# A two-phase recurrent recommender: the length mask moves to gathered rows, one exponential and one transpose move ahead, and some index columns are fetched earlier

## The chip, the cores and the metric

The kernel runs on one core of a Trainium2 chip. A core has five engines with instruction queues of their own, each of which works strictly in the order of its queue: TensorE (PE; PEld is its weight loads), VectorE (DVE), ScalarE (ACT), GpSimd (POOL) and SyncE (SP), which here issues most of the transfers. Engines wait for one another through semaphores. The metric is the device time of one execution in microseconds, the median of several runs.

## The reference

1024 users each have a history of 100 item vectors of 128 numbers, a 0/1 mask of 100 entries, and a length from 1 to 100. In float32:

1. A GRU runs over the 100 items; its states are the `keys` (1024 x 100 x 128).
2. Each key gets a score by a small network of the key, the item and their product. A softmax over the masked scores gives `attn`, and `pooled = sum over t of attn * keys` (1024 x 128).
3. `att_seq = pooled.T[:100]`: an entry of a *user's* pooled vector at feature t serves as the attention weight of another user at step t, through the transposition that the reference makes.
4. A second recurrence (AUGRU) runs over the keys: `u = a_t * sigmoid(..)`, `h = (1 - u) * h + u * tanh(..)`. Of its 100 states, the one at position length - 1 is used.
5. That state, the user, the item, a masked history mean and their product go through a three-layer network with sigmoids to one number per user.

```python
att_seq = pooled.T[:T]
u = a_t[:, None] * u
h_new = (1.0 - u) * h + u * h_hat
attention_feature = jnp.take_along_axis(aug_out, idx, axis=1)[:, 0, :]
```

Since only the state at length - 1 counts, a weight of zero from there on freezes the state. So the kernel sets the weights of steps at or past a user's length to zero (the mask of lengths, `used`), sorts the users by length, longest first, and lets the second recurrence become narrower as users drop out.

## The kernel before

**Phase 1** (`gru_phase`). 1024 users are two halves of 512 columns; features lie on the 128 partitions. A loop over t = 0..99 runs the GRU step of each half (24 matmuls with 128 x 32 weights each, `gru`), scores the keys of the step before (`attend`, `take`), runs the softmax in blocks of steps as *stages* (`softmax`: scores, tops, then `exponents`, then sums), and lets POOL add up the masked history and the pooled keys. Keys are transposed on DVE in 32 x 32 blocks and stored to DRAM in `keys_d`, whose rows hold 8 steps each (4 in the first). The order of every queue is written out by hand: there is no planner.

Work for later is a generator, `load_later`: at each step of the loop that has no softmax stage, it advances to its next `yield`. It loads lengths and masks, ranks the users (each step one comparison of 1024 elements, `above`), scatters identity and place by rank into a DRAM table `inv_d`, reads it back sorted into `idx` and `idx_k` (the row numbers for later gathers), and makes the masks `used` and `used_first`, and `quad` and `low`, small columns that pick a partition's own quarter.

**The hand-over.** After the loop (from about 1372 us of the profile) the last scores, the last softmax blocks and the features of the final network are worked off. `features(g)` alternates matmuls and an ACT copy to `part` (L720); `some(6, 7)` advances features 6 and 7. `key(n, half)` transposes the keys of steps 0 and 1. Then the pooled values of the first four features (`soon`) are finished, multiplied with `used_first` into `first_w` (L1089), and sorted by two matmuls, `by_row` (L1099) and `first` (L1105), which give the state after step 0 (L1114). After that the pooled values of the other features (`rest`) are finished on DVE, multiplied with `used` (L1122) and stored by SP to `pooled_d` (L1125). At the end every engine loads the word `over_d` and branches (L1587, L1588) to one of three versions of phase 2 that differ in their widths.

**Phase 2** (`augru_phase`) runs steps 1 to 99. Up to a narrow width, each step is two `half_step(t, i)`, i = 0, 1. In such a half step PE closes `ph` of the half step before, closes `pr` and `pu` of this one, and opens three gates of the next one (`open_gates`, L1239), which needs that one's keys `k`; DVE makes `r` (L1275), the new `h` (L1277), `pu * at` (L1281) and `rest` (L1284). `load_key(t, i)` puts the keys of a step on the features' side: for t < 4 by PE, later by a DVE transpose (L1228) of rows that POOL gathers from `keys_d` by an indirect DMA (`load_row`, L189). Before such a gather, POOL copies one column of a DVE result into the row's buffer (`later["pace"]`, L188), so that gathers keep pace with the steps. The weights are gathered by POOL from `pooled_d` (`gather_weights`, L154); `store_weights` transposes them on PE (L1188, at the end of half steps (2, 1) and (3, 0)), DVE copies them out (L1190), and SP stores them to `att_d`, from where each step's row is loaded (`load_att`, L1203). `predict` is the final network, for groups of users as they drop out.

What sets the order around the change: in half step (4, 0) the keys of (4, 1) are transposed, after `rest` and right before the gates of (4, 1) are opened:

```python
if (t, i) == (FIRST[1], 0):   # FIRST[1] is 4
    load_key(t, 1)
```

Of the kernel before, what the change touches and what calls it, by code (L numbers as in the profile page):

```python
# [9 lines left out]
F32 = mybir.dt.float32  # L10
# [9 lines left out]
P = 128  # L20
B = 1024
# [63 lines left out]
def kernel(ctx: ExitStack, tc: tile.TileContext, a: dict, out: bass.AP):  # L85
# [34 lines left out]
    mask_d = dram.tile([T, B], BF16, name="mask_d")  # L120
    inv_d = dram.tile([B, 2], I32, name="inv_d")
    perm_d = dram.tile([NH, 2, HB], F32, name="perm_d")
# [16 lines left out]
    pooled = const.tile([P, NK, R], F32, name="pooled")  # L139
    idx = const.tile([P, GH, NH * 2], I32, name="idx")  # L140
    idx_k = const.tile([P, KH, NH], I32, name="idx_k")
    quad = const.tile([P, SOON], F32, name="quad")
    idx_p = const.tile([P, HB // PR], I32, name="idx_p")
    h_all = const.tile([P, NH, HB], F32, name="h_all")
# [7 lines left out]
    def gather(dst, src, g, i):  # L152

        nc.gpsimd.indirect_dma_start(  # L154
            out=dst,
            out_offset=None,
            in_=src,
            in_offset=bass.IndirectOffsetOnAxis(ap=idx[:, g, 2 * i : 2 * i + 1], axis=0),
        )
# [40 lines left out]
    def gru_phase(pools):  # L200
# [72 lines left out]
        def load_later():  # L273
# [30 lines left out]
            nc.gpsimd.iota(step_i, pattern=[[1, T]], base=0, channel_multiplier=0)  # L304
            ids = pre.tile([P, NG, 2], I32, name="ids")
            nc.gpsimd.iota(ids[:, :, 0], pattern=[[P, NG]], base=0, channel_multiplier=1)
# [16 lines left out]
            own = pre.tile([P, NG], F32, name="own")  # L323
            nc.scalar.copy(own, ids[:, :, 0])
            room = []
            for j, room_i in enumerate(rooms):
# [69 lines left out]
            nc.vector.tensor_scalar_mul(low[:, 0:1], r3, -3.0)  # L396
            nc.vector.tensor_scalar_mul(low[:, 1:2], r3, -3.0 * R)
            nc.vector.tensor_scalar_mul(r3, r3, -3.0)
            yield
            for c in range(SOON):  # L400
                nc.vector.tensor_scalar(
                    quad[:, c : c + 1], quarter, float(c * R), None, ALU.is_equal
                )
            yield
# [7 lines left out]
                out=own, in0=length, scalar=float(B), in1=own, op0=ALU.mult, op1=ALU.subtract  # L412
            )
            yield
            rank = pre.tile([P, NG], F32, name="rank")
            rank_i = pre.tile([P, NG], I32, name="rank_i")
            for g in range(NG):
# [10 lines left out]
                yield  # L428
            nc.vector.tensor_copy(rank_i, rank)
            for g in range(NG):  # L430
                nc.gpsimd.indirect_dma_start(
                    out=inv_d,
                    out_offset=bass.IndirectOffsetOnAxis(ap=rank_i[:, g : g + 1], axis=0),
                    in_=ids[:, g, :],
                    in_offset=None,
                )
                yield
# [5 lines left out]
            for i in range(NH):  # L443
# [3 lines left out]
                )  # L447
            place_i = pre.tile([P, KH, NH, 2], I32, name="place_i")
            len_k = pre.tile([P, NK], I32, name="len_k")
# [11 lines left out]

            own_place = pre.tile([P, GH, NH * 2], F32, name="own_place")
            nc.scalar.copy(own_place, idx)
            yield
            parts = pre.tile([P, 2, NH, GH], F32, name="parts")
            for i in range(NH):
                at_id, at_place = (own_place[:, :, 2 * i + j] for j in range(2))
                nc.vector.scalar_tensor_tensor(
                    out=parts[:, 0, i],
                    in0=at_id,  # L470
                    scalar=float(P // R),
                    in1=at_place,
                    op0=ALU.mult,
                    op1=ALU.subtract,
                )
                nc.vector.tensor_sub(parts[:, 1, i], at_place, at_id)
            yield
            for i in range(NH):
# [603 lines left out]
        for half in halves:  # L1082
# [6 lines left out]
        nc.vector.tensor_mul(  # L1089
            w.rearrange("p (c k) -> p k c", c=SOON),  # L1090
            pooled[:, :, soon],
            later["used_first"].rearrange("p c k -> p k c"),
        )
# [25 lines left out]
        for half in reversed(halves):  # L1119
            half.pool(T, nc.vector, rest)  # L1120
            acc = pooled[:, half.ks, :]
            nc.vector.tensor_mul(acc, acc, later["used"][:, half.ks, :])  # L1122
            to = pooled_d[half.cols, :].rearrange("(k r) f -> r k f", r=R)
# [8 lines left out]
    def augru_phase(pools, widths, alive):  # L1132
# [50 lines left out]
        def store_weights(i):  # L1183

            n = T - SOON
            p = pa.tile([P, HB], F32, tag="a", name="pw")
            for g in range(GH):
                nc.tensor.transpose(p[:n, ts(g, P)], sorted_rows[i][:, g, SOON:T], ident)  # L1188
# [65 lines left out]
        def half_step(t, i):  # L1254
# [54 lines left out]

            if (t, i) == (FIRST[1] - 1, 0):  # L1310
                load_key(t + 1, i)
# [77 lines left out]
        def predict(g, last=False):  # L1389
# [80 lines left out]
            for q in range(P // R):  # L1470
# [6 lines left out]
                )  # L1477
            all_y = later["all_y"]
            nc.vector.tensor_add(all_y, p, all_y)
            nc.sync.dma_start(  # L1480
                out=out.rearrange("(q c) -> q c", c=BQ),
                in_=all_y.rearrange("(q r) c -> q r c", r=R)[:, 0, :],
            )

# [16 lines left out]
        def earlier_results():  # L1501
            later["all_y"] = wp.tile([P, BQ], F32, tag="att_t", name="all_y", bufs=2)
            nc.sync.dma_start(
                out=later["all_y"],
                in_=early_d.rearrange("(q c) o -> q (o c)", c=BQ)
                .unsqueeze(1)
                .to_broadcast([P // R, R, BQ]),
            )
# [152 lines left out]
```

## Time and profile before

| | |
|---|---|
| median of 3 runs | 2004.55 us (2002.19 to 2005.18) |
| the profiled execution | 2006.11 us |
| its span, first to last instruction | 2004.3 us |
| mean granted clock of PE | 0.997 of full |
| busy PE / DVE / POOL / ACT | 1983.5 / 1679.0 / 1263.7 / 942.9 us |

The span is shorter than the time of its own execution by 1.8 us, which lies before the first and after the last instruction. All times below that are written like 1422.72 are microseconds from the start of the span. Busy time counts work only: waits, branches and the issuing of transfers are not in it. In the order of instructions, neighbours of one kind are joined (x4); float32 matmuls come as two passes. What stands in brackets is the engine's idle time before an instruction and what, by the semaphores, ended it; where several semaphores are waited for, it is the one that came last by the profile, which need not be the cause.

### The profile page before, as it was taken

To read this page: it belongs to the slowest core of one execution; us is meant where nothing else is said; L and a number is where in the kernel's file an instruction comes from. 1 tells how busy PE (TensorE), PEld (TensorE's weight loads), DVE (VectorE), ACT (ScalarE), POOL (GpSimd) and SP (SyncE) were. 2 spreads that over 40 slices of the span, in tenths; PEclk is the share of its full clock that TensorE was granted. 3 is DMA by queue.
4 is the path that set the end of the run, shared out by engine and by line. 5 is a ranking of instruction groups with operands and counts; after the bars stand their busy time and mean duration, and the time that the engine had idled before them with its cause. 6 is when DMAs were issued, how large, how long until landed. Compare 5 with 4: busy or idle time off the path is not lost.

```text
span 2004.3 us, 40958 instructions
## 1 busy us (share of the span) xinstructions
PE 1983.5 (99%) x15324; PEld 954.9 (48%) x15324; DVE 1679.0 (84%) x3038; ACT 942.9 (47%) x1690; POOL 1263.7 (63%) x1307
## 2 busy tenths in 40 slices
PE   9999999999999999999999999999899999999998
PEld 2345555555333333333333333345344556678997
DVE  7888989897978888888878798998677778888995
ACT  4444454454544444544444444546333444445563
POOL 0333939568796959596896868898753454445331
PEclk9999999999999999999999999999999999999999
DMA  4443333323333533333333333332542333333331
GB/s 125 98 118 92 107 106 101 93 86 102 115 106 109 117 100 117 118 114 100 104 111 107 107 92 107 103 96 77 157 130 90 101 107 98 93 103 99 84 82 33
DMA packets 244300, 205.59 MB, mean 103 GB/s; under 512 B 61538, under 2 KB 206794, under 8 KB 244090
## 3 DMA queue, kind: packets, MB, share of 16 engines
q1 hardware_dynamic: 231578, 170.29, 29.6%
q0 software_dynamic: 12224, 32.04, 5.7%
q8 instruction: 123, 2.02, 0.4%
q14 instruction: 87, 0.71, 0.1%
q10 hardware_dynamic: 288, 0.52, 0.1%
HBM read 146.73 MB, written 54.42 MB: 100 GB/s over the span
## 4 chain that ended last, share of the span: by engine, by line
PE 95%; DVE 1%; POOL 1%; DMA 1%; ACT 1%; issue 1%; SPq 0%; POOLq 0%; DVEq 0%; ACTq 0%
PE ps L569 50%; PE pm L745 17%; PE ph L1243 4%; PE pr L1239 4%; PE ph L1239 4%; PE pu L1239 4%; PE pu L1243 4%; PE pr L1243 4%; DMA rows<-keys_d,idx_k 1%; POOL rows L189 1%; PE last L712 1%; PE pr L1334 0%; PE ph L1334 0%; POOL att_r L154 0%; PE p L1454 0%
## 5 line engine op out<-in xcount | busy, mean ns | idle before, releaser
L569 PE MATMUL ps<-x,wih 128*32 128x512 f32 x4800 | 653.1, 593 | 0.0
L569 PE MATMUL ps<-hn,whh 128*32 128x512 f32 x4752 | 646.3, 592 | 1.6 <-ACT hn L617 1.6
L569 PEld LDWEIGHTS ps<-x,wih 128*32 128x32 f32 x4800 | 212.1, 110 | 315.1 <-issue 285.8
L569 PEld LDWEIGHTS ps<-hn,whh 128*32 128x32 f32 x4752 | 209.7, 110 | 311.9 <-issue 302.8
L554 POOL TENSOR_TENSOR xm<-x,m 128x512 f32<-128x512 f32 x200 | 235.8, 1179 | 143.0 <-DMA m<-mask_d 142.7
L581 ACT ACTIVATE r<-ps,brz 128x512 f32<-128x512 f32 x200 | 137.7, 689 | 387.6 <-PE ps L569 387.1
L555 POOL TENSOR_TENSOR hist<-hist,xm 128x512 f32<-128x512 f32 x200 | 257.7, 1289 | 15.7
L189 POOL DMA_INDIRECT rows<-keys_d,idx_k x218 | 211.9, 972 | 84.5 <-POOL rows L188 73.6
L675 POOL TENSOR_TENSOR pooled<-pooled,kw 128x512 f32<-128x512 f32 (+1 forms) x191 | 244.0, 1278 | 15.0
L674 POOL TENSOR_TENSOR kw<-kt,e 128x512 f32<-128x512 f32 (+1 forms) x191 | 205.1, 1074 | 67.1 <-DVE e L863 67.0
L600 ACT ACTIVATE ps<-ps,bih 128x512 f32<-128x512 f32 x200 | 132.4, 662 | 226.8 <-DVE ps L599 226.8
L745 PE MATMUL pm<-hn,wk 128*32 128x512 f32 x1200 | 228.8, 592 | 0.0
L745 PE MATMUL pm<-kq,wkq 128*32 128x512 f32 x1200 | 228.7, 592 | 0.0
L1251 ACT ACTIVATE c<-ph,bh 128x510 f32<-128x510 f32 (+57 forms) x174 | 88.3, 507 | 258.4 <-PE ph L1243 258.3
L745 PE MATMUL pm<-mv,w 128*32 128x512 f32 (+1 forms) x808 | 207.8, 592 | 0.0
L589 DVE SCALAR_TENSOR_TENSOR u<-ps,bhh,r 128x512 f32<-128x512 f32 x198 | 147.6, 745 | 69.4 <-PE ps L569 65.4
L604 DVE TENSOR_TENSOR d<-hn,ps 128x512 f32<-128x512 f32 x198 | 136.2, 688 | 35.5 <-ACT ps L600 35.3
L188 POOL COPY rows<-rest 128x1 f32<-128x1 f32 x198 | 37.5, 189 | 197.9 <-DVE rest L1284 196.5
L617 ACT COPY hn<-ps 128x512 f32<-128x512 f32 x200 | 116.5, 583 | 93.2 <-DVE kq L611 91.4
L605 DVE TENSOR_TENSOR d<-ps,d 128x512 f32<-128x512 f32 x200 | 138.4, 692 | 25.6 <-ACT ps L601 11.6
L599 DVE TENSOR_TENSOR ps<-ps,u 128x512 f32<-128x512 f32 x200 | 140.0, 700 | 22.7 <-PE ps L569 2.0
L1273 DVE TENSOR_TENSOR pu<-pu,c 128x510 f32<-128x510 f32 (+57 forms) x173 | 82.0, 474 | 80.7 <-ACT c L1251 78.5
(263 smaller groups left out, 3164.2 us busy)
## 6 DMA issues: line engine op xcount, KB each, us to landing
x<-in_hist_x SPq DMA_DIRECT2D x210, 256.0 KB
keys_d<-kt SPq DMA_DIRECT2D x48, 1024.0 KB
m<-mask_d SPq DMA_DIRECT2D x200, 128.0 KB
rows<-keys_d,idx_k POOLq DMA_INDIRECT x218, 3.0
s_b<-mv SPq DMA_DIRECT2D x200, 8.0 KB
keys_d<-kt SPq DMA_DIRECT2D x32, 64.0 KB
mask_i<-in_mask SPq DMA_DIRECT2D x8, 200.0 KB
part_d<-part SPq DMA_DIRECT2D x2, 400.0 KB
```

The source lines that it names most:

```text
L189: nc.gpsimd.indirect_dma_start(out=r[:, at, :], out_offset=None, in_=keys_d[q], in_offset=bass.IndirectOffsetOnAxis(ap=idx_k[:, k, i : i + ...
L554: nc.gpsimd.tensor_mul(d, x, m)
L555: nc.gpsimd.tensor_add(acc, acc, d)
L569: nc.tensor.matmul(p[ts(q, R), :], lhsT=w[:, g, ts(q, R)], rhs=v, start=(j == 0), stop=(j == len(parts) - 1),)
L589: nc.vector.scalar_tensor_tensor(out=u, in0=ph, scalar=bhh[:, 2:3], in1=r, op0=ALU.add, op1=ALU.mult,)
L599: nc.vector.tensor_add(pi, pi, u)
L605: nc.vector.tensor_mul(d, pz, d)
L674: eng.tensor_mul(d, k, w)
L675: eng.tensor_add(acc, acc, d)
L745: nc.tensor.matmul(p[i][s, :], lhsT=w[:, s], rhs=v, start=start, stop=stop)
L1239: nc.tensor.matmul(p, lhsT=m[:, 1, :], rhs=k, start=True, stop=False)
L1243: nc.tensor.matmul(p, lhsT=m[:, 0, :], rhs=v, start=False, stop=True)
```

## The change

- The exponential of the last softmax block (`stage(2); exponents()`) is issued ahead of the second `some(6, 7)`, whose part on ACT is two copies.
- `used` shrinks to the first four steps and a quarter of the partitions each, and replaces `used_first`; `first_w` is laid out as (k c) instead of (c k). The two multiplies of `pooled` with `used` (L1122) are gone.
- In their place `used_s`, a mask in the sorted order, is made in phase 1 from a third column of `inv_d` (the length), and `store_weights` multiplies the gathered rows with it on DVE before PE transposes them.
- `quad` and a column of `low` now come from two small index columns, made by POOL, stored to DRAM (`kc_d`) and loaded back across the partitions one stage of `load_later` later (`kc_p`), well before they are used.
- Keys of step 4: in step 3, each half step transposes its own half's; before, the second half's were transposed in (4, 0).
- In steps 1 and 2 gathers have no pacing copy.
- The results' buffer `all_y` lies in `pooled`, and the last store is issued after the generator of the last prediction instead of at its end.
- `load_later` has three `yield`s fewer.

```diff
+    kc_d = dram.tile([2, P], I32, name="kc_d")
-    idx = const.tile([P, GH, NH * 2], I32, name="idx")
+    idx = const.tile([P, GH, NH * 3], I32, name="idx")
+    used_s = const.tile([P, NH, GH, T - SOON], U8, name="used_s")
+    all_y = pooled.rearrange("p k r -> p (k r)")[:, :BQ]
...
+            nc.gpsimd.tensor_copy(ids[:, :, 2], len_i)
...
-            nc.vector.tensor_scalar_mul(low[:, 1:2], r3, -3.0 * R)
             nc.vector.tensor_scalar_mul(r3, r3, -3.0)
-            yield
-            for c in range(SOON):
-                nc.vector.tensor_scalar(
-                    quad[:, c : c + 1], quarter, float(c * R), None, ALU.is_equal
-                )
+            kc = mid.tile([1, 2, NK, SOON], I32, name="kc", **once)
+            nc.gpsimd.iota(
+                kc[:, 0], pattern=[[1, NK], [0, SOON]], base=0, channel_multiplier=0
+            )
+            nc.gpsimd.iota(
+                kc[:, 1], pattern=[[0, NK], [1, SOON]], base=0, channel_multiplier=0
+            )
+            nc.sync.dma_start(
+                out=kc_d.rearrange("j p -> (j p)").unsqueeze(0),
+                in_=kc.rearrange("o j k c -> o (j k c)"),
+            )
             yield
...
+            kc_p = pre.tile([P, 2], I32, name="kc_p")
+            nc.sync.dma_start(out=kc_p, in_=kc_d.rearrange("j p -> p j"))
             yield
...
+            kc_f = pre.tile([P, 2], F32, name="kc_f")
+            nc.scalar.copy(kc_f, kc_p)
+            nc.vector.tensor_scalar_mul(low[:, 1:2], kc_f[:, 0:1], -3.0 * R)
+            for c in range(SOON):
+                nc.vector.tensor_scalar(
+                    quad[:, c : c + 1], kc_f[:, 1:2], float(c), None, ALU.is_equal
+                )
...
+                nc.vector.tensor_tensor(
+                    out=used_s[:, i],
+                    in0=own_place[:, :, 3 * i + 2].unsqueeze(2).to_broadcast([P, GH, T - SOON]),
+                    in1=step[:, SOON:].unsqueeze(1).to_broadcast([P, GH, T - SOON]),
+                    op=ALU.is_gt,
+                )
...
-            column = pre.tile([P, R], F32, name="column")
-            nc.vector.tensor_scalar(column, step[:, :R], quarter, None, ALU.add)
-            yield
-            used_first = later["used_first"] = pre.tile([P, SOON, NK], U8, name="used_first")
-            used = later["used"] = pre.tile([P, NK, R], U8, name="used")
+            used = later["used"] = pre.tile([P, NK, SOON], U8, name="used")
             nc.vector.tensor_tensor(
                 out=used,
-                in0=last.unsqueeze(2).to_broadcast([P, NK, R]),
-                in1=column.unsqueeze(1).to_broadcast([P, NK, R]),
+                in0=last.unsqueeze(2).to_broadcast([P, NK, SOON]),
+                in1=step[:, :SOON].unsqueeze(1).to_broadcast([P, NK, SOON]),
                 op=ALU.is_gt,
             )
-            yield
-            nc.vector.tensor_scalar(
-                used_first.rearrange("p c k -> p k c"), used[:, :, :SOON], quad[:, 0:1], None, ALU.mult
-            )
+            nc.vector.tensor_scalar(quarter, quarter, 0.0, None, ALU.is_equal)
+            nc.vector.tensor_scalar(used, used, quarter, None, ALU.mult)
             yield
...
-        some(6, 7)
         stage(2)
         exponents()
+        some(6, 7)
...
         nc.vector.tensor_mul(
-            w.rearrange("p (c k) -> p k c", c=SOON),
-            pooled[:, :, soon],
-            later["used_first"].rearrange("p c k -> p k c"),
+            w.rearrange("p (k c) -> p k c", c=SOON), pooled[:, :, soon], later["used"]
         )
...
             half.pool(T, nc.vector, rest)
-            acc = pooled[:, half.ks, :]
-            nc.vector.tensor_mul(acc, acc, later["used"][:, half.ks, :])
...
             p = pa.tile([P, HB], F32, tag="a", name="pw")
+            later_rows = sorted_rows[i][:, :, SOON:T]
+            nc.vector.tensor_mul(later_rows, later_rows, used_s[:, i])
             for g in range(GH):
...
-            later["pace"] = rest[:, 0:1]
+            later["pace"] = rest[:, 0:1] if t > SOON - 2 else None
...
-            if (t, i) == (FIRST[1], 0):
-                load_key(t, 1)
...
-            if (t, i) == (FIRST[1] - 1, 0):
+            if t == FIRST[1] - 1:
                 load_key(t + 1, i)
...
         all_of(final)
+        nc.sync.dma_start(
+            out=out.rearrange("(q c) -> q c", c=BQ),
+            in_=all_y.rearrange("(q r) c -> q r c", r=R)[:, 0, :],
+        )
```

More of the change, by code (lines that the diff above doesn't have):

```diff
@@ L120 @@
     mask_d = dram.tile([T, B], BF16, name="mask_d")
-    inv_d = dram.tile([B, 2], I32, name="inv_d")
+    inv_d = dram.tile([B, 3], I32, name="inv_d")
+    kc_d = dram.tile([2, P], I32, name="kc_d")
     perm_d = dram.tile([NH, 2, HB], F32, name="perm_d")
@@ L157, in gather @@
             in_=src,
-            in_offset=bass.IndirectOffsetOnAxis(ap=idx[:, g, 2 * i : 2 * i + 1], axis=0),
+            in_offset=bass.IndirectOffsetOnAxis(ap=idx[:, g, 3 * i : 3 * i + 1], axis=0),
         )
@@ L304, in load_later @@
             nc.gpsimd.iota(step_i, pattern=[[1, T]], base=0, channel_multiplier=0)
-            ids = pre.tile([P, NG, 2], I32, name="ids")
+            ids = pre.tile([P, NG, 3], I32, name="ids")
             nc.gpsimd.iota(ids[:, :, 0], pattern=[[P, NG]], base=0, channel_multiplier=1)
@@ L447, in load_later @@
                 )
-            place_i = pre.tile([P, KH, NH, 2], I32, name="place_i")
+            place_i = pre.tile([P, KH, NH, 3], I32, name="place_i")
             len_k = pre.tile([P, NK], I32, name="len_k")
@@ L460, in load_later @@
             nc.vector.tensor_scalar(idx_k, place_i[:, :, :, 1], quarter, None, ALU.add)
-            own_place = pre.tile([P, GH, NH * 2], F32, name="own_place")
+            own_place = pre.tile([P, GH, NH * 3], F32, name="own_place")
             nc.scalar.copy(own_place, idx)
@@ L466, in load_later @@
             for i in range(NH):
-                at_id, at_place = (own_place[:, :, 2 * i + j] for j in range(2))
+                at_id, at_place = (own_place[:, :, 3 * i + j] for j in range(2))
                 nc.vector.scalar_tensor_tensor(
@@ L1477, in predict @@
                 )
-            all_y = later["all_y"]
             nc.vector.tensor_add(all_y, p, all_y)
[L1480 to L1483, printed above, removed]
         def last_places():
@@ L1501, in earlier_results @@
         def earlier_results():
-            later["all_y"] = wp.tile([P, BQ], F32, tag="att_t", name="all_y", bufs=2)
             nc.sync.dma_start(
-                out=later["all_y"],
+                out=all_y,
                 in_=early_d.rearrange("(q c) o -> q (o c)", c=BQ)
```

## The prediction

> **What bounds the kernel now.** I read the page's busy line and chain first, then busy time by stretch, then the order of instructions wherever TensorE (PE) idles.
>
> ```profile
> PE 1983.5 (99%) x15324; PEld 954.9 (48%) x15324; DVE 1679.0 (84%) x3038; ACT 942.9 (47%) x1690; POOL 1263.7 (63%) x1307
> PE 95%; DVE 1%; POOL 1%; DMA 1%; ACT 1%; issue 1%; SPq 0%; POOLq 0%; DVEq 0%; ACTq 0%
> ```
>
> PE sets the time; only its 2004.3 - 1983.5 = 20.8 us of idleness can be won. The stretches (length, then busy time of PE, PEld, DVE, ACT, POOL, clock, DMA) show where it lies:
>
> ```profile
> 100.00:1330.00 1230.00, 1229.43 (x11464) 486.23 (x11460) 1063.23 (x1621) 582.95 (x935) 904.98 (x769) 1.00 0.35 104
> 1396.00:1413.00 17.00, 12.52 (x52) 7.37 (x50) 13.60 (x35) 7.08 (x13) 13.38 (x16) 1.00 0.40 116
> 1425.00:1458.00 33.00, 32.33 (x92) 14.50 (x90) 19.53 (x32) 14.39 (x23) 26.14 (x40) 1.00 0.57 162
> 1458.00:1466.00 8.00, 4.81 (x8) 2.08 (x8) 3.79 (x7) 0.66 (x2) 4.73 (x9) 0.79 0.61 203
> ```
>
> Phase 1 has no idle PE, so index and mask work there is covered. The hand-over to phase 2 and the start of step 4 have some. The order of instructions in the hand-over (start, duration, engine, line; in brackets the idle time before and its releaser):
>
> ```profile
> 1400.00 0.33 ACT L720 COPY part<-last 128x200 f32<-128x200 f32 x1 [1.03 <-PE last L712]
> 1400.22 0.24 ACT L860 ACTIVATE last<-last 128x96 f32<-128x96 f32 x1
> 1403.99 1.13 DVE L1089 TENSOR_TENSOR first_w<-pooled,used_first 128x128 f32<-128x128 f32 x1 [0.40 <-POOL pooled L659]
> 1407.50 1.98 PE L1105 MATMUL first<-s_b,quad 128*128 128x512 f32 x4 [0.32 <-DVE s_b L1101]
> 1412.95 1.45 PE L1239 MATMUL pr<-hist,wr 128*128 128x510 f32 x2 [3.47 <-issue]
> 1418.02 0.69 DVE L1122 TENSOR_TENSOR pooled<-pooled,used 128x512 f32<-128x512 f32 x1
> 1422.72 0.69 DVE L1275 TENSOR_TENSOR r<-h_all,pr 128x510 f32<-128x510 f32 x1 [4.02 <-DMA rows<-keys_d,idx_k]
> 1423.46 1.12 PE L1243 MATMUL ph<-r,wh 128*128 128x510 f32 x2 [1.22 <-DVE r L1275]
> ```
>
> The DMA named before `r` is not the cause. The lines of the branch show DVE loading `over_d` and branching at 1419.0, and its first instruction, a semaphore wait, at 1422.2. PE has the same hole: branch at 1409.0, next work 1412.95. So each engine crosses the branch by itself, some 3 to 4 us after its last phase-1 work; DVE is last, and PE's first closing of `ph` waits for it.
>
> Steps 2 to 4:
>
> ```profile
> 1444.07 0.69 DVE L1284 SCALAR_TENSOR_TENSOR rest<-pu,h_all 128x506 f32<-128x506 f32 x1
> 1444.56 0.60 PE L1188 MATMUL pw<-ident,att_r 128*96 128x128 f32 x4
> 1451.35 0.97 POOL L189 DMA_INDIRECT rows<-keys_d,idx_k  x1 [0.27 <-POOL rows L188]
> 1455.13 0.68 DVE L1284 SCALAR_TENSOR_TENSOR rest<-pu,h_all 128x500 f32<-128x500 f32 x1
> 1457.24 0.69 DVE L1273 TENSOR_TENSOR pu<-pu,c 128x500 f32<-128x500 f32 x1 [1.43 <-ACT c L1251]
> 1460.00 0.68 DVE L1284 SCALAR_TENSOR_TENSOR rest<-pu,h_all 128x496 f32<-128x496 f32 x1
> 1460.59 1.35 DVE L1228 STREAM_TRANSPOSE k<-rows 128x512 f32<-128x512 f32 x3
> 1461.34 1.99 PE L1239 MATMUL pr<-k,wr 128*128 128x496 f32 x2 [3.19 <-DVE k L1228]
> ```
>
> PE idles 3.19 us for the keys of step 4, second half. The chain puts a gather ahead of that transpose, but the rows concerned were issued at 1451.35, and gathers here land in 3.4 us (median): they were there by about 1455. The transpose begins just as `rest` of (4, 0) ends: it is late in DVE's order.
>
> [...] after the 3.19 us hole three matmuls (pr, ph, pu) take from 1461.34 to 1465.64, 4.30 us, where the three from 1455.49 to 1457.16 start 0.83 us apart, so 2.49 for three: 1.8 us lost. [...]
>
> **The change, part by part.**
>
> *Exponential ahead of the copies.* Its input is ready at about 1399.15 and ACT is free from 1398.98, but it stands behind a copy that waits for PE until 1400.00, and runs at 1400.22. Ahead of it, it runs at about 1399.2: 1.0 us for DVE and POOL, down to `first_w`, now at about 1402.95. The two copies wait for PE anyway and the copies of key 1 (1400.49) stay put: no cost.
>
> *`first_w` in another layout.* 1.13 us for 128 elements; 64-element neighbours take 0.22, so it becomes 0.3 if the strided layout made it slow, or stays. Either way the next bound is PE: the gate matmuls ahead of `by_row` leave room from about 1404.67 instead of the 1405.23 seen. From there, in the seen durations: `by_row` ends 1.02 us later (1405.69) and the first `s_b` starts at 1405.8 (seen 1406.76, behind three DVE operations that now end by 1405.0 to 1405.9). The rest follows by the seen spacing, so DVE's and PE's last phase-1 work moves up by 0.97; I take 0.95. With the slow layout it is 0.85.
>
> *`pooled` no longer masked.* Two L1122, one 0.61 and one 0.66 us apart from their successors: DVE reaches its branch 1.27 sooner. Together `r` moves from 1422.72 to about 1420.5, so `ph` could start at 1421.2. PE's own earlier work, ending now with room at 1422.1, moves by 0.95 to 1421.15. Both agree; `ph` goes from 1423.46 to 1421.2: **-2.2 us**. If the branch took longer, the gain would shrink towards 0.95, not below it.
>
> *Mask on gathered rows.* Two DVE multiplies of 4x96 = 384 elements: [...] 0.53 to 0.69 by the rows of 448 and 512. They stand behind `rest` (starts 1444.07, successor 0.6 later): 1444.67 to 1445.23, then a handshake of 0.05, so the `pw` transposes start at 1445.3 instead of 1444.56. PE is in order: `ph` of (2, 1) and all after it wait 0.75. In (3, 0) the same: `rest` 1449.60, `pw` 1450.04 becomes 1450.8. No cover: **+1.5 us** (0 if PE had other slack, 1.8 with the longer multiply). Their rows were gathered by 1438, so no wait for a DMA.
>
> *Keys of step 4 in step 3.* The transpose (0.69) now follows `rest` of (3, 1), 1455.13 + 0.6, into DVE's 1.43 us wait for `c`. Queued behind it: `pu*c`, `r`, `h`; none delayed if the rows are there. The hole goes: **-3.2 us**, and with it the half clock, -1.8 here. [...] I count **-1.4** (estimate, bounds 0 and 1.8).
>
> *No pacing copy in steps 1 and 2.* Twelve POOL copies of 0.19 ahead of the gathers of these rows. The `pooled_d` stores start 1.5 us sooner, so do the weight gathers; with 12x0.19 = 2.3 the last row is issued near 1448.5 to 1449 and lands near 1452, 3 us before its new use. At the worst landing in the stretch (6.7) it would be 1455.5: just in time. Nothing by itself.
>
> *Index columns, phase 1.* inv_d rows of 12 bytes, not 8; two small POOL iotas, one store, one load of 256 four-byte elements, a copy, a few DVE operations; two comparisons of 384 elements [...] in, one of 1024 with its followers out. SP's store waits for POOL, whose queue at that point (222 us) is about a step behind, due at about 227, when SP has its next own store. PE has 0.57 us of idle time in 1230 us although DVE already has a 4 us burst at 222: 0. If the cover failed, 1 to 2 us. The output buffer in `pooled` and the moved last store keep their places in the queues: 0.
>
> Sum: -2.2 +1.5 -3.2 -1.4 = -5.3. The profiled execution took 2006.11 (span 2004.3), which gives 2000.8; the runs' median is 2004.55, 1.6 below it, and gives **1999.2**.
>
> **Rivals.** *The gather takes the stall's place*: the transpose sits in DVE's queue from 1455 and waits. For: gathers issued at 1455.67 landed only at 6.7 us, beside the `at` loads. Against: these rows are issued 6 us earlier. Landing at 1459.5 gives a hole like the old one: 2004.55 -2.2 +1.5 = 2003.9. *It ends slower*: the same wait, with `pu*c`, `r` and `h` behind it. Each us after 1456 is a us of PE; the hole from about 1457.4 costs its length plus 1.8. A row landing at 1465 gives 1465.7-1457.4+1.8 = 10.1 in place of 5.0: 2004.55 -0.7 +5.1 = 2009.0. It decides from about 1460. *DVE becomes the bound, or the branch does not move*: the multiplies cost 1.8, the hand-over gives 0.95, the clock nothing: 2004.55 -0.95 +1.8 -3.2 = 2002.2. *Multiplies hidden*: 1999.2 - 1.5 = 1997.7, or with the full clock 1997.3.
>
> **Chances.** Forecast (1997.5 to 2000.5) 0.70; multiplies hidden 0.04; smaller gains 0.12; gather in the stall's place 0.08; slower 0.06. A measurement of this kernel can tell about 0.2% (4.0 us) from no change. Faster 0.74, same 0.20, slower 0.06. The range 1996.5 to 2004.0 holds all but the slower case and some tails; the forecast's own is 1997.5 to 2000.5.
>
> **What would show it.** Right: no hole before the opening of `pr` of (4, 1), full clock there; the k transpose of 512 directly behind `rest` of (3, 1); `r` of (1, 0) about 2 us sooner; 0.7 us holes before both `pw`; the exponential ahead of the last two `part` copies. Wrong: a DVE wait for rows in (3, 1), idle PE in phase 1, or a new wait behind the branch.

## The result, and the profile after

| | median, runs (range) | kernel before, beside it | ratio, 95% interval |
|---|---|---|---|
| the changed kernel | 1997.63 us, 6 (1997.1 to 1998.9) | 2004.87 us, 6 (2002.19 to 2007.81) | 0.9964 (0.9951 to 0.9977) |
| the same once more, on another chip | 1998.53 us, 7 (1998.05 to 1998.67) | 2004.23 us, 11 (2002.35 to 2008.13) | 0.9972 (0.9960 to 0.9983) |

The change made the kernel 0.3 to 0.4% faster, 5.7 to 7.2 us, where 5.3 were forecast. On one further chip three close variants of it (I, J and K below) were slower than the kernel before. The profiled execution has a span of 1995.9 us instead of 2004.3. First its busy line and its chain, then busy time by stretch for the same four stretches as before (PE, PEld, DVE, ACT, POOL, clock, DMA share, GB/s):

```profile
PE 1978.6 (99%) x15324; PEld 1277.6 (64%) x15324; DVE 1674.6 (84%) x3040; ACT 942.9 (47%) x1691; POOL 1262.6 (63%) x1298
PE 97%; DVE 1%; ACT 1%; issue 0%; DMA 0%; POOL 0%; DVEq 0%; ACTq 0%; POOLq 0%
```
```profile
100.00:1330.00 1230.00, 1230.00 (x11474) 817.61 (x11470) 1059.72 (x1624) 582.78 (x936) 906.32 (x771) 1.00 0.35 104
1396.00:1413.00 17.00, 13.46 (x51) 7.71 (x50) 14.51 (x37) 6.85 (x13) 13.93 (x17) 1.00 0.44 129
1425.00:1458.00 33.00, 31.24 (x89) 14.30 (x88) 20.41 (x35) 12.83 (x20) 24.43 (x30) 1.00 0.53 156
1458.00:1466.00 8.00, 8.00 (x21) 3.70 (x20) 6.46 (x12) 3.09 (x5) 4.86 (x9) 1.00 0.57 192
```

The last stretch is the find: PE is busy 8.00 of 8 us at full clock, where it was 4.81 at 0.79 (0.52 from 1461.34 to 1463.33 us, right behind the hole). The third, with the two new multiplies in it, has lost a little: 31.24 us of work instead of 32.33.

The hand-over, in order of instructions:

```profile
1398.46 0.23 ACT L878 ACTIVATE last<-last 128x96 f32<-128x96 f32 x1 [1.20 <-DVE last L872]
1399.34 0.33 ACT L738 COPY part<-last 128x200 f32<-128x200 f32 x1 [0.40 <-PE last L730]
1402.45 0.97 POOL L682 TENSOR_TENSOR pooled<-pooled,e 128x448 f32<-128x448 f32 x1
1402.52 1.04 DVE L1107 TENSOR_TENSOR first_w<-pooled,used 128x128 f32<-128x128 f32 x1 [0.70 <-POOL pooled L677]
1405.20 1.41 DVE L1117 TENSOR_TENSOR s_b<-by_row,block 128x512 f32<-128x512 f32 x2
1411.11 1.12 PE L1255 MATMUL pr<-hist,wr 128*128 128x510 f32 x2 [3.19 <-issue]
1419.52 0.69 DVE L1291 TENSOR_TENSOR r<-h_all,pr 128x510 f32<-128x510 f32 x1 [3.71 <-DMA pooled_d<-pooled]
1420.26 1.12 PE L1259 MATMUL ph<-r,wh 128*128 128x510 f32 x2 [1.56 <-DVE r L1291]
```

The exponential now waits for its input alone and stands ahead of the copies. The holes at the branch are still there, 3.19 us on PE and 3.71 on DVE (3.47 and 4.02 before), and `ph` of (1, 0) waits for DVE's `r` here. `first_w` still takes 1.04 us.

Steps 2 to 4, in order:

```profile
1440.80 0.69 DVE L1300 SCALAR_TENSOR_TENSOR rest<-pu,h_all 128x506 f32<-128x506 f32 x1
1441.40 0.55 DVE L1202 TENSOR_TENSOR att_r<-att_r,used_s 128x384 f32<-128x384 f32 x1
1442.05 0.61 PE L1204 MATMUL pw<-ident,att_r 128*96 128x128 f32 x4 [0.53 <-PE pu L1255]
1448.27 0.61 PE L1204 MATMUL pw<-ident,att_r 128*96 128x128 f32 x4 [0.57 <-PE pu L1255]
1453.31 0.68 DVE L1300 SCALAR_TENSOR_TENSOR rest<-pu,h_all 128x500 f32<-128x500 f32 x1
1453.90 0.70 DVE L1244 STREAM_TRANSPOSE k<-rows 128x512 f32<-128x512 f32 x1
1456.23 0.99 PE L1255 MATMUL pr<-k,wr 128*128 128x496 f32 x2
```

Two holes of 0.53 and 0.57 us have come ahead of the `pw` transposes, behind a multiply of 0.55 us each; the one of 3.19 us ahead of `pr` of (4, 1) is gone, and the transpose of its keys stands directly behind `rest` of (3, 1).

**Stage by stage.** Instructions that both kernels have can be laid beside each other. The table says by how much the median shift of ACT's and DVE's instructions, against the kernel before, changed over each stage; "end" is what is left to the difference of the spans. Those of the experiments below stand in it too. Phase 1 is up to 1395 us, the hand-over to 1425, steps 2 and 3 to 1457, step 4 to 1470.

| kernel | phase 1 | hand-over | steps 2, 3 | step 4 | end |
|---|---|---|---|---|---|
| changed | -0.62 | -2.58 | +1.44 | -5.15 | -1.5 |
| changed, second profile | -0.63 | -2.39 | +1.45 | -5.15 | -1.4 |
| A keys alone | -0.60 | -0.10 | 0.00 | -5.15 | +0.2 |
| B keys back | +0.60 | -2.28 | +1.45 | -0.20 | -1.1 |
| C pacing kept | +0.24 | -2.56 | +1.58 | -5.15 | -1.1 |
| D rows unmasked | +0.44 | -2.08 | 0.00 | -5.15 | -0.8 |
| E mask earlier | +1.22 | -2.04 | 0.00 | -5.15 | -1.4 |
| F POOL takes a part | +0.68 | -2.90 | +1.48 | -5.16 | 0.0 |
| G E and F | +0.77 | -1.14 | 0.00 | -5.15 | -1.4 |
| H E, pacing kept | -0.88 | -2.39 | +0.01 | -2.24 | -1.0 |

Phase 1 scatters by 2 us between profiles whatever the edit. The end is half clock and closing work: in the profile of before the last small matmuls ran at half clock (0.50 granted from 1999.40 to 2000.60 us), 0.63 us each, in the changed kernel's first they took 0.38 to 0.40 us at 1.00, and POOL's closing instructions took 0.4 us less. Whether that is chance alone is open. From the end of DVE's last `h_all` to the end of the span, the two profiles without the moved last store (before and A) took 8.21 and 8.11 us, eleven of the twelve with it 6.72 to 7.17 us, and F 8.06 us. The store follows DVE's last addition by 0.45 us in both kernels, and no run moves it alone. The profiled execution of before was also 1.2 us slower than the median of its six runs (2006.11 against 2004.87 us), so the table shows more than the medians do. What was forecast to move stands in the middle three columns, which sum to -6.3 and -6.1 us in the changed kernel's two profiles.

### The profile page after: what moved, and what is told of

Read it like the earlier page. It is cut to its first block, busy times and chain, and to the rows that moved or that the text cites. A ratio compares the mean times of both kernels' runs of the same rounds, so it can differ in the third digit from the quotient of the medians.

```text
span 1995.9 us, 40934 instructions
## 1 busy us (share of the span) xinstructions
PE 1978.6 (99%) x15324; PEld 1277.6 (64%) x15324; DVE 1674.6 (84%) x3040; ACT 942.9 (47%) x1691; POOL 1262.6 (63%) x1298
## 3 DMA queue, kind: packets, MB, share of 16 engines
q8 instruction: 123, 2.02, 0.4%
## 4 chain that ended last, share of the span: by engine, by line
PE 97%; DVE 1%; ACT 1%; issue 0%; DMA 0%; POOL 0%; DVEq 0%; ACTq 0%; POOLq 0%
PE ps L587 51%; PE pm L763 18%; PE ph L1259 5%; PE ph L1255 4%; PE pu L1259 4%; PE pr L1259 4%; PE pu L1255 4%; PE pr L1255 4%; PE pr L1348 0%; PE last L730 0%; PE ph L1348 0%; PE p L1468 0%; ACT pr L1367 0%; PE pd L247 0%; DVE r L1375 0%
## 5 line engine op out<-in xcount | busy, mean ns | idle before, releaser
L587 PE MATMUL ps<-x,wih 128*32 128x512 f32 x4800 | 727.5, 593 | 0.0
L587 PE MATMUL ps<-hn,whh 128*32 128x512 f32 x4752 | 721.3, 592 | 1.3 <-ACT hn L635 1.3
L587 PEld LDWEIGHTS ps<-x,wih 128*32 128x32 f32 x4800 | 350.3, 110 | 192.7 <-issue 41.1
L587 PEld LDWEIGHTS ps<-hn,whh 128*32 128x32 f32 x4752 | 347.7, 110 | 189.5 <-issue 36.8
L763 PE MATMUL pm<-hn,wk 128*32 128x512 f32 x1200 | 255.2, 592 | 0.0
L763 PE MATMUL pm<-kq,wkq 128*32 128x512 f32 x1200 | 255.0, 592 | 0.0
L763 PE MATMUL pm<-mv,w 128*32 128x512 f32 (+1 forms) x808 | 195.9, 592 | 0.1
```

What stands on the lines that cost most here:

```text
L587: nc.tensor.matmul(p[ts(q, R), :], lhsT=w[:, g, ts(q, R)], rhs=v, start=(j == 0), stop=(j == len(parts) - 1),)
L763: nc.tensor.matmul(p[i][s, :], lhsT=w[:, s], rhs=v, start=start, stop=stop)
```

## The experiments

Each group of kernels ran on one chip, beside the kernel before.

### A and B: the keys of step 4, alone and taken back

A is the kernel before with this edit only; B is the changed kernel with it undone:

```diff
-            if (t, i) == (FIRST[1], 0):
-                load_key(t, 1)
-            if (t, i) == (FIRST[1] - 1, 0):
+            if t == FIRST[1] - 1:
                 load_key(t + 1, i)
```

> The kernel before, with only the keys of step 4 transposed in step 3. My theory: the 3.19 us of idle TensorE ahead of the opening of pr of (4, 1) goes, and with it the half clock behind it (1.4 to 1.8 us): 2004.9 - 4.8 = 2000.1 us, range 1999.5 to 2001.7 (the latter if the half clock was luck). Its last rows are issued at about 1451.4 and land at about 1454.4 us, ahead of the transpose at 1455.7. Rival (the gather takes the stall's place): the transpose waits for rows until about 1459, the hole stays, 2004 to 2005 us. Neither the hand-over (r of (1, 0) at 1422.7) nor the pw transposes should move.

> The changed kernel with the second half's keys of step 4 back in step 4. My theory: a hole of about 3.2 us returns ahead of pr of (4, 1), and a half clock of about 1.8 us behind it [...]: 1997.6 + 3.2 = 2000.8 us without, 2002.6 us with. Rival (this part was worth nothing, what the rows' earlier gathers brought is the gain): 1997.6 us, and the hole much shorter than 3.2 us.

A: 2000.46 us (9 runs) against 2005.78 (24 runs), ratio 0.9973 (0.9963 to 0.9982). B: 2004.61 us (14 runs) against the same, 0.9995 (0.9987 to 1.0003). From A, the transpose and PE's opening of the gates:

```profile
1454.43 0.68 DVE L1284 SCALAR_TENSOR_TENSOR rest<-pu,h_all 128x500 f32<-128x500 f32 x1
1455.03 0.70 DVE L1228 STREAM_TRANSPOSE k<-rows 128x512 f32<-128x512 f32 x1
1457.29 0.99 PE L1239 MATMUL pr<-k,wr 128*128 128x496 f32 x2
```

From B, PE at the same place:

```profile
1461.04 2.02 PE L1255 MATMUL pr<-k,wr 128*128 128x496 f32 x2 [3.12 <-DVE k L1244]
1462.86 1.69 PE L1255 MATMUL ph<-k,wh 128*128 128x496 f32 x2
1464.38 1.00 PE L1255 MATMUL pu<-k,wu 128*128 128x496 f32 x2
```

The moved keys alone bring most of the change, 5.15 us of the 6.1 to 6.3 in the middle columns, and without them little is left of it: B's time cannot be told from that of the kernel before. In B the hole is back, 3.12 us, and the half clock with it: `pr` and `ph` take (2.02 - 0.99) + (1.69 - 0.99) = 1.73 us more than at full clock. The gather did not take the stall's place. B came out 2 us above its expectation, which was made from the first chip's 1997.6. Phase 1, 1.2 us later in B's profile than in the changed kernel's first, and the chip, on which the kernel before takes 0.9 us more, are of that size together.

### C: the pacing copies kept

```diff
-            later["pace"] = rest[:, 0:1] if t > SOON - 2 else None
+            later["pace"] = rest[:, 0:1]
```

> The changed kernel with the pacing copies of steps 1 and 2 kept. My theory: their removal was worth nothing by itself: 1997.6 us (within 0.5). The last row of step 4 is issued 1 to 3 us later than the 1448.4 us of the changed kernel, lands by about 1454, and the transpose still begins within 1 us of rest of (3, 1). Rival (removing the copies was what kept the gather out of the stall's place): the transpose in (3, 1) waits several us for rows, a hole of 2 us or more returns ahead of pr of (4, 1), 1999.6 us or more.

1999.21 us (8 runs) against 2005.78, ratio 0.9972 (0.9961 to 0.9982): the same as the changed kernel, and none of the middle three stages differs by more than 0.15 us from it. But the margin is not the same. The last row for these keys is issued at 1451.41 us instead of 1448.41 and lands at 1454.50; the transpose begins at 1454.99. In the changed kernel it landed at 1451.20, 2.7 us ahead of the transpose. H shows what that margin is for.

### D and E: the multiplies of the gathered rows, taken away and moved

D leaves the two multiplies out, and with them the mask of lengths from step 4 on. E moves them half a step ahead of their use:

```diff
+            if (t, i) in ((2, 0), (2, 1)):
+                later_rows = sorted_rows[i][:, :, SOON:T]
+                nc.vector.tensor_mul(later_rows, later_rows, used_s[:, i])
...
-            later_rows = sorted_rows[i][:, :, SOON:T]
-            nc.vector.tensor_mul(later_rows, later_rows, used_s[:, i])
```

> The changed kernel without the two multiplies of the gathered rows; it leaves out the mask of lengths from step 4 on. My theory: each multiply holds TensorE for 0.7 us, so both pw transposes start about 0.05 us behind the gate matmuls ahead and the time falls by 1.4 us to 1996.2 us. Rival (they stand beside another wait of equal length, for the rows or for a bank): the gaps before pw stay and the time is 1997.6 us.

> The changed kernel with each of the two multiplies one half step earlier: that of the first half behind rest of (2, 0), where DVE then waits 2.05 us for c, that of the second behind rest of (2, 1), where it waits 0.75 us for pw. My theory: the rows landed before, the multiplies are covered, and the time falls by 1.4 us to 1996.2 us with all the work done. Rival (a wait moves in: the rows of a half are not there yet, and pu*c, r and h stand behind the multiply): no gain or slower, 1997.6 us or more, with a DVE wait for rows in step 2.

D: 1998.68 us (6 runs), ratio 0.9966 (0.9954 to 0.9978); E: 1998.22 us (5 runs), 0.9960 (0.9946 to 0.9974), both against 2005.72 (11 runs). DVE and PE in E:

```profile
1438.32 0.55 DVE L1313 TENSOR_TENSOR att_r<-att_r,used_s 128x384 f32<-128x384 f32 x1
1440.45 0.69 DVE L1287 TENSOR_TENSOR pu<-pu,c 128x506 f32<-128x506 f32 x1 [1.58 <-ACT c L1265]
1442.90 1.00 PE L1253 MATMUL pu<-k,wu 128*128 128x500 f32 x2
1443.74 0.60 PE L1202 MATMUL pw<-ident,att_r 128*96 128x128 f32 x4
```

The multiply takes 0.55 us out of DVE's wait for `c` (1.58 us left, 2.05 in D), and `pw` follows the gate matmul after 0.84 us, with no hole. In the stages the multiplies cost 1.44 us where they stood and nothing half a step earlier: the cost was in their place, not in their work. The medians do not show it (1998.2 and 1998.7 instead of the expected 1996.2): phase 1 was 1.1 to 1.8 us later in these two profiles than in the changed kernel's. E should beat the changed kernel by 1.4 us; the timed runs don't prove that it does.

### F and G: DVE's last work ahead of the branch given to POOL

F lets POOL do the first half's last multiply and add; G is F and E together:

```diff
-        halves[0].pool(1, nc.gpsimd, rest)
+        halves[0].pool(T, nc.gpsimd, rest)
```

> The changed kernel with the last multiply and add of the first half's pooling (128x448 each) on POOL instead of DVE. My theory: DVE's arrival at the branch alone sets the start of step 1, so r of (1, 0) comes 1.3 us sooner (1418.2 instead of 1419.5), TensorE idles 0.3 instead of 1.56 us before ph, and the time falls by 1.25 us to 1996.4 us. Rival 1 (DVE's start behind the branch is set [...] by something that does not move with its arrival): r stays at 1419.5, 1997.6 us. Rival 2 (POOL's 2.2 us more delay its gathers and these become late in step 3 or 4): slower than 1997.6 us.

> The changed kernel with both edits, the early multiplies and the pooling on POOL. My theory: the two gains lie in different stretches and add up, 1.4 + 1.25: 1995.0 us. Rival (POOL's later gathers reach DVE, whose early multiplies or transposes then wait for rows): 1996.2 us or more.

F: 1999.87 us (6 runs), ratio 0.9969 (0.9957 to 0.9981); G: 1999.18 us (5 runs), 0.9960 (0.9947 to 0.9974), against 2005.72. No gain: a miss. DVE came sooner in F as expected, by 1.34 us at its last operation and 1.25 us at `r`, once phase 1's shift is taken out. But PE did not wait for it any more: the hand-over gains 0.3 to 0.5 us more than in the changed kernel in F, and 1.3 to 1.4 us less in G. PE in G:

```profile
1412.83 2.07 PE L1253 MATMUL pr<-hist,wr 128*128 128x510 f32 x2 [3.47 <-issue]
1414.69 1.91 PE L1253 MATMUL pu<-hist,wu 128*128 128x510 f32 x2
1416.39 1.91 PE L1257 MATMUL pr<-h_all,wr 128*128 128x510 f32 x2
1423.20 1.02 PE L1257 MATMUL ph<-r,wh 128*128 128x510 f32 x2
```

From `pr` to `ph` PE works without a hole, 10.4 us in G. In the changed kernel's first profile the same matmuls took 7.4 us (1411.11 to about 1418.5) at full clock. The difference is half clock behind PE's hole at the branch. Granted clock from 1409 to 1423 us, in the first changed profile, in its second, and in G:

```profile
1409.00:1423.00 14.00, 10.33 (x27) 4.58 (x28) 9.12 (x16) 3.84 (x6) 8.77 (x10) 1.00 0.68 162
```
```profile
1409.00:1423.00 14.00, 11.81 (x26) 5.11 (x27) 9.08 (x15) 3.71 (x6) 8.79 (x10) 0.88 0.70 166
```
```profile
1409.00:1423.00 14.00, 10.53 (x21) 4.54 (x21) 8.56 (x14) 2.49 (x4) 10.62 (x12) 0.76 0.58 131
```

0.88 of 14 us is a deficit of 1.7 us, 0.76 one of 3.4. Of the 14 profiles of this study two have 1.00 here, nine 0.88 and three 0.76. PE idled more than 0.3 us ahead of this `ph` in only three of the 14: before (1.22 us), the changed kernel's first (1.56) and I (2.15). So PE's own work behind the branch is usually the bound, or level with DVE, and the first profile was an exception. In the second profile of the changed kernel DVE's `r` was ready just when PE was:

```profile
1419.71 0.69 DVE L1291 TENSOR_TENSOR r<-h_all,pr 128x510 f32<-128x510 f32 x1 [3.87 <-DMA rows<-keys_d,idx_k]
```
```profile
1419.46 1.02 PE L1255 MATMUL pu<-hist,wu 128*128 128x510 f32 x2
1420.45 1.12 PE L1259 MATMUL ph<-r,wh 128*128 128x510 f32 x2
```

### H: the mask earlier and the pacing kept, beside the changed kernel

```diff
-            later["pace"] = rest[:, 0:1] if t > SOON - 2 else None
+            later["pace"] = rest[:, 0:1]
+            if (t, i) in ((2, 0), (2, 1)):
+                later_rows = sorted_rows[i][:, :, SOON:T]
+                nc.vector.tensor_mul(later_rows, later_rows, used_s[:, i])
...
-            later_rows = sorted_rows[i][:, :, SOON:T]
-            nc.vector.tensor_mul(later_rows, later_rows, used_s[:, i])
```

> The changed kernel with the multiplies of the gathered rows half a step earlier and the pacing copies of steps 1 and 2 kept. My theory: 1.4 us faster than the changed kernel run beside it (the multiplies are covered, the pacing is worth nothing): 1996.2 us where that one takes 1997.6. Should the run fall where ScalarE and TensorE stall in steps 2 and 3 for 14 us with their inputs ready, as in the profiles with the copies first, the two extra operations and the gathers first: if the unpaced gathers cause those stalls, this kernel's are shorter by at least 4 us than the changed kernel's; if not (rival), both have the same stalls and differ by 1.4 us only.

> The changed kernel as it is, beside the kernel before and the one with early multiplies and pacing. My theory: 1997.6 us (1996.6 to 1999.6, as phase 1 alone varies by 1 to 2 us between profiles), ratio 0.996 to before; TensorE's half clock behind the branch, absent in its first profile, may be there and then costs 0.5 to 1.5 us. Rival: the gain of the first comparison was luck of the clock, and the ratio is 0.998 or more. Where the stalls of 14 us show, 2018 to 2020 us, and above the kernel before.

H: 1997.73 us (5 runs, 1996.96 to 1999.56), ratio 0.9966 (0.9952 to 0.9979); the changed kernel 1998.53 us, both against 2004.23 (11 runs). The difference is 0.8 us where 1.4 was expected, and the two ranges overlap. The stalls that the expectation speaks of (those of the last group, below) did not show. The early multiplies are covered again, but the profile has something that neither expectation had:

```profile
1451.87 0.68 DVE L1298 SCALAR_TENSOR_TENSOR rest<-pu,h_all 128x500 f32<-128x500 f32 x1
1456.78 0.71 DVE L1242 STREAM_TRANSPOSE k<-rows 128x512 f32<-128x512 f32 x1 [4.23 <-DMA rows<-keys_d,idx_k]
1457.54 1.10 PE L1253 MATMUL pr<-k,wr 128*128 128x496 f32 x2 [2.65 <-DVE k L1242]
```

Here the gather did take the stall's place. With the pacing copies the last row is issued at 1450.94 and lands at 1456.65, 5.7 us later, while the steps now want it at 1452.5. Had it landed in C's 3.1 us, it would still have come 1.5 us late (an estimate from these times). So the removal of the copies is worth nothing by itself (C), and in this profile, beside faster steps 2 and 3, it would have been worth 2.9 us (2.24 instead of E's 5.15 in step 4). The profiled execution is the slowest of H's five, so this wait need not be in the other four; the timed runs do not tell E and H apart (ratios 0.9960 and 0.9966).

### I, J and K: the exponential, the masks of `pooled`, and `first_w`

I puts the last two copies ahead of the exponential again, J puts two operations of the removed multiplies' size back, K lets POOL issue two gathers ahead of its last tensor operations:

```diff
 I
+        some(6, 7)
         stage(2)
         exponents()
-        some(6, 7)
 J
             half.pool(T, nc.vector, rest)
+            acc = pooled[:, half.ks, :]
+            nc.vector.tensor_max(acc, acc, acc)
 K
+        gather_early(2)
         halves[0].pool(1, nc.gpsimd, rest)
```

> The changed kernel with the last two feature copies ahead of the exponential again. My theory: the exponential runs 1.0 us later, first_w too, and the first s_b and all of DVE up to the branch 0.7 to 0.95 us later: 1998.3 to 1998.6 us. Rival (the exponential was not on the way to first_w, POOL's share of the pooling or TensorE is): s_b stays at 1405.2, 1997.6 us.

> The changed kernel with two more DVE operations of 128x512 on pooled (the maximum of it with itself, so nothing changes) where the two multiplies by the mask of lengths stood. My theory: they put back 1.3 us ahead of DVE's branch: r of (1, 0) at about 1420.8 instead of 1419.5, and the time rises by 1.3 us to 1998.9 us. Rival (those multiplies were hidden, since TensorE crosses the branch as late or the start behind it does not follow DVE's arrival): r stays, 1997.6 us.

> The changed kernel with two of POOL's key gathers ahead of its last pooling operations, so that POOL runs no tensor operation while DVE runs first_w. My theory: first_w takes 1.04 us for 128 elements because POOL's operation of 0.97 us holds it; without it, it takes about 0.3 us, and the time stays at 1997.6 us (within 0.5), since by_row waits for TensorE then. Rival (its layout of strided columns is slow): first_w stays at 1.0 us.

These three met a chip on which the kernel before too is 11 us slower: 2016.35 us (24 runs, 2013.39 to 2020.45). Against it I took 2021.75 us (7 runs, ratio 1.0023, 1.0012 to 1.0035), J 2022.40 (6 runs, 1.0032, 1.0020 to 1.0044), K 2020.27 (17 runs, 1.0023, 1.0016 to 1.0030). All three are slower than before there, which no expectation had. I take the hand-over first, where the chip changes little.

I, DVE behind the exponential:

```profile
1400.30 0.23 DVE L881 TENSOR_TENSOR last<-last,on 128x64 f32<-128x64 f32 x1 [1.41 <-ACT last L878]
1406.77 1.28 DVE L1117 TENSOR_TENSOR s_b<-by_row,block 128x512 f32<-128x512 f32 x2
```

With phase 1's shift taken out, `s_b` and DVE's last operation are 1.05 us later than in the changed kernel. In J, DVE's two extra operations and `r`:

```profile
1415.58 0.69 DVE L1138 TENSOR_TENSOR pooled<-pooled 128x512 f32<-128x512 f32 x1
1417.57 0.69 DVE L1138 TENSOR_TENSOR pooled<-pooled 128x512 f32<-128x512 f32 x1
1422.35 0.69 DVE L1293 TENSOR_TENSOR r<-h_all,pr 128x510 f32<-128x510 f32 x1 [4.09 <-issue]
```

DVE's last operation ends 1.29 us later, `r` comes 1.67 later (the hole at the branch was 4.09 us instead of 3.71). Up to DVE's last operation both parts have about the size that was forecast. `r` comes 1.7 us later in I too, as its hole at the branch is 4.37 us. K, DVE and POOL around `first_w`:

```profile
1404.57 0.29 DVE L1107 TENSOR_TENSOR first_w<-pooled,used 128x128 f32<-128x128 f32 x1 [0.69 <-POOL pooled L677]
```
```profile
1404.22 0.32 POOL L677 TENSOR_TENSOR pooled<-pooled,kw 128x64 f32<-128x64 f32 x1
1404.69 1.04 POOL L192 DMA_INDIRECT rows<-keys_d,idx_k  x1
```

Without a tensor operation of POOL beside it (the gather begins 0.12 us behind it), `first_w` takes 0.29 us, not 1.04, in the same layout. So the new layout is not its cost; the old one was not run this way. The hand-over gains nothing by it (-2.56 in K, -2.58 in the changed kernel's first profile), since PE is the next bound there.

**What stays open.** On this chip most of the loss lies in steps 2 and 3: 13.9 to 16.5 us more than in the first profile of before, 1.4 of it the multiplies. Another 4.5 to 6.2 us are lost in a few places between 1847 and 1981 us, while step 4 (-5.15) gains as elsewhere. ACT in K:

```profile
1435.64 0.66 ACT L1285 ACTIVATE pu<-pu,bu 128x506 f32<-128x506 f32 x1
1447.58 0.58 ACT L1239 COPY k<-pk 128x500 f32<-128x500 f32 x1 [11.27 <-remote]
1450.40 0.68 ACT L1268 ACTIVATE c<-ph,bh 128x506 f32<-128x506 f32 x1 [2.25 <-remote]
1453.93 0.66 ACT L1284 ACTIVATE pr<-pr,br 128x506 f32<-128x506 f32 x1 [2.85 <-PE pu L1256]
```

PE's matmuls that write `pk` are recorded as ended by 1438.6 us, those that close `ph` by 1439.4. But the updates of PE's semaphore that the copy and `c` wait for are recorded only at 1447.55 and 1450.38, 0.02 to 0.03 us ahead of the two (`remote` in the brackets is a sender that the profile could not tell). In the changed kernel's own profile PE's updates at this place come within 0.1 us of its matmuls' ends. So what came late here, by 9 and 11 us, is PE's signal, or its record.

POOL issued gathers without a pause from 1436.3 to 1451.0 in this time, unpaced. That fits a delay by these gathers, but the losses after 1847 us lie where the gathers are paced, and H, which was to tell, fell on another chip. The DMA queues that the profile names `instruction` show nothing unusual: from 1405 to 1465 us they moved 13 packets in K and 13 in the changed kernel's own profile. The recording may have a part: the traces of I, J and K hold 22,251 to 22,355 updates of semaphores where the other eleven hold 25,501 to 25,527, and only 56 to 58 in the stretch from 1434 to 1455 us where those have 400 to 458.

The kernel before was not profiled on this chip, so where its own 11 us lie is not known, and the changed kernel itself was not run there. As K's edit moves no other stage, it is likely slower than the kernel before on such a chip. That is argued, not shown.

## Why the prediction was right, and where not

**Keys of step 4 (-3.2, and -1.4 for the clock).** Right in the cause: the rows were there, the transpose was late in DVE's order. A and B show it from both sides. The clock's term, an estimate of the author's, was too small: both profiles with the hole, before and B, lose 1.7 to 1.8 us to half clock behind it, and the stage gave 5.15 us, not 4.6. The rival of a gather in the stall's place fell for the changed kernel, and came true for H.

**No pacing (0).** Right as a number, as C shows. The last row was issued at 1448.41 and landed at 1451.20 (forecast 1448.5 to 1449, and 1452). The step did not say that the copies' removal buys the margin which covers any faster step 2 or 3.

**Row mask (+1.5).** Right: a multiply of 0.55 us each, +1.44 together, by D and E. No other slack hid them.

**Hand-over (-2.2).** Right, -2.4 to -2.6 in the two profiles: the exponential 1.05 (0.95 forecast, by I), the multiplies 1.29 (1.27, by J), and in the first profile a hole at the branch that was 0.3 us shorter on DVE than before, which no term forecast. "Both agree" turned out to be the sentence that mattered: PE, with the usual half clock behind its hole (0.88 granted over 14 us in nine of 14 profiles), is level with DVE, so F gained nothing although the first profile showed 1.56 us of PE waiting for DVE. On `first_w` the prediction left two cases open, layout or not; neither named POOL, without whose tensor operation beside it `first_w` took 0.29 us in K.

**Phase 1 and the end (0).** The first profile shows -0.6 and -1.5 there. A, which has neither the index columns nor the moved store, has the same -0.6 in phase 1 (all profiles lose a wait of 0.57 us at 516.8 us that only the first profile of before had), so the index work is hidden as said. The end was put at nothing; 0.8 to 1.5 us of half clock and closing work came off it in the profiles with the moved store, F apart, and whether the edit has a part in that is open. These and the clock's term are why the first comparison gave 7.2 us; the second, 5.7, is nearer to the sum.

**Level.** Carrying the sum over to the median of three runs of before was right: 1999.2 forecast, 1997.63 and 1998.53 measured. The first of these lies at the edge of the forecast's range and on the number of the rival "multiplies hidden" (1997.7), so the total alone does not decide between the two, and that it fell inside the range is in part luck. The profiles decide: D and E show the multiplies' 1.44 us.

## What to carry to other kernels

A stall whose data is already there is a question of order: move the producer into a slot where its engine waits anyway, and then look at how much earlier the data is than the new slot, because the next improvement eats that margin. Where two engines cross a gate almost together, a profile that shows one of them waiting is one draw; before giving its work away, ask what the other costs at half clock (here 10.4 us instead of 7.4). And gains of a microsecond in two milliseconds are read by laying the traces beside each other stage by stage: here phase 1 alone moved the total by more than most edits.

## What was not expected of the hardware

- **A small DVE operation slower beside POOL.** `first_w` took 1.04 to 1.13 us beside a POOL tensor operation of about 1 us, and 0.29 us without one (K). In the changed kernel POOL's operation began at 1402.45 and took 0.97 us; `first_w` began at 1402.52 and ended at 1403.56, just behind it. Not every DVE operation is held so: the next one, of 128x448 at 1403.48, took 0.61 us beside POOL's next (1403.37, 1.02 us). Beside a gather it did not show: in the same profile a subtraction of 128x96 in the softmax (L872) took 1.35 us beside a POOL tensor operation (at 1346.16) and 0.25 us beside a gather (at 1382.05). Why is not shown.
- **Half clock behind holes of about 3 us was the rule here, not luck.** Holes of 2.96 to 3.68 us at the branch were followed by half clock in 12 of 14 profiles, and in three of them the deficit was twice that of the others (3.4 us of 14 instead of 1.7). The length of the hole does not decide it: the changed kernel's second profile had 3.25 us and then 0.88 over the 14 us, I had 3.25 us and then 1.00. A hole of 2.65 us (H) was not followed by half clock: the matmuls behind it took 1.10, 0.99 and 0.99 us.
- **Gathers slow down by place, not by kernel.** Where landings are recorded, row gathers mostly land in 2.7 to 3.5 us (131 of 171 in the changed kernel, 99 of 146 in the one before); those issued from about 1452.4 to 1457 us, beside the loads of `at`, mostly in 4 to 6.8 us, in the changed kernel (6.78 us at 1452.74, 6.35 at 1454.75) and in the one before (3.77 at 1452.79, 6.67 at 1455.67). In H one issued at 1450.94 took 5.7 us already.
